# Stores in four transfers, and earlier loads of network vectors and bias rows, in a two-layer generated-weight convolution

## The chip, the cores and the metric

The kernel runs on one core of one Trainium2 chip. The metric is the device time of one execution in microseconds (us). "us" without more is a time of the profiled execution, counted from the start of its span.

## The reference, cut to what matters

Two layers of the same form follow each other. Each normalizes its input, makes a convolution kernel for every position from a small network, applies it, and adds the result and a bias to its input. Sizes: S = 32 samples, B = 32 chunks, C = 64 channels, L = 256 positions, A = 16, H = 128, all float32.

```python
x = x + conv(_gn(x), layer 0);  x = x + conv(_gn(x), layer 1)

def _gn(v, G=32, eps=1e-5):            # groups of 8 positions, over B and C too
    m, s = mean, var of v over (chunk, channel, 8 positions)
    return (v - m) / sqrt(s + eps)

def conv(x, z, W1, b1, g1, be1, W2, b2, Wb1, bb1, gb1, beb1, Wb2, bb2):
    h = relu(_ln(z @ W1 + b1, g1, be1))
    w = (h @ W2 + b2).reshape(B, L, CI, CO, K)       # K = 3 taps
    hb = relu(_ln(z @ Wb1 + bb1, gb1, beb1))
    bias = (hb @ Wb2 + bb2).transpose(0, 2, 1)
    x_uf = x padded by 1, three shifts stacked
    return einsum('sbilk,bliok->sbol', x_uf, w) + bias[None]
```

## The kernel before

**First stage** (`first_stats`, lines 223 to 290). The input goes through on-chip memory once, in 16 transfers of 4 MB, for the statistics of layer 0 (VectorE). Beside it 32 slots run the two small networks of both layers, two chunks per slot: class `Hidden` loads z (`zt`, line 163), projects (line 168), squares, sums and takes the root (ScalarE, GpSimd), transposes (line 195) and writes the hidden vectors to `hd` (line 201) and the bias rows to `bd` (line 216), both in device memory. All these transfers are issued by SyncE's queue (SP).

**Main loop** (lines 499 to 516). 64 units u (32 chunks in each of two layers) are done in two halves of the output channels, so that v = 2u + h runs from 0 to 127. In a half, TensorE makes the convolution kernels from `hT` (the hidden vectors of the unit, line 112) and `w2` in 12 groups (`make`, lines 418 and 419), and VectorE adds `b2` and puts them into `wall` (`take`, line 431). `products(v)` (lines 448 and 457) multiplies them with the normalized input `xn` and adds the result to the residual `ys[v % 3]`, in which GpSimd has added the bias rows `bt` to the input (`add_bias`, line 388). In layer 0 VectorE also takes the statistics of the result (line 460). After the first group of half v + 1 follow `products(v)` and then `after(v)`, in this order:

- `store(v)`: the finished half (1 MB, runs of 256 bytes) from `ys[v % 3]` to `x1` or `out`, issued by ScalarE's queue (line 397), in transfers of 8 partitions where u is even and of 4 where u is odd: 16 or 32 for a half.
- `normalize` (line 408): GpSimd subtracts `gmean` from `xt` into `xn`, and multiplies by `rstd` there.
- `load_pairs` (lines 122 and 123): the next input into `xt`, 2 MB in two transfers, SP. They wait for the subtraction, which reads `xt`.
- `load_residual(v + 3)` (line 131): 1 MB in four transfers, SP. Each waits for the stores that read the same part of the ring of three.
- `add_bias(v + 3)`: four transfers of `bt` (line 384, 1 MB written), SP, then the addition on GpSimd.

`load_hidden(u + 1)` (line 114, SP) stands at the start of the second half of unit u, behind all of this for the half before it. `hT` has two buffers, `bt` one.

What sets the order: instructions run in the order written on each engine, and a queue's issues wait in line. Besides the waits for data, each transfer is given one of eight semaphores (DMAHW0 to DMAHW7) in turn, over both queues together, and waits until the transfer that had the same semaphore before, eight transfers earlier, has landed.

Of the kernel before, what the change touches and what calls it, by code (L numbers as in the profile page):

```python
# [23 lines left out]
FP = mybir.dt.float32  # L24
# [17 lines left out]
def conv_layers(ctx: ExitStack, tc: tile.TileContext, x: bass.AP, layers: list, out: bass.AP):  # L42
# [18 lines left out]
    BLK = 2 * L  # L61
    NBLK = BLK // P
    RING = 3
    assert 2 * C == P and NT * S == P and M == P and BLK == 512 and EB == 2 * E
# [47 lines left out]
    def load_hidden(u):  # L112
        h = hp.tile([P, 2, M], FP, tag="hT", name="hT")
        nc.sync.dma_start(out=h, in_=hd[u // 2][u % 2].rearrange("p (a m) -> p a m", a=2))
        return h
# [41 lines left out]
    class Hidden:  # L157


        def __init__(self, stage, zts, small, i):  # L160
            n, j = divmod(i, B // 2)
            self.stage, self.i, self.t, self.zt = stage, i, small[n], zts[i % len(zts)]
            nc.sync.dma_start(out=self.zt[0:A], in_=layers[n]["z"][:, j * BLK : (j + 1) * BLK])

# [18 lines left out]
        def scale(self):  # L183
# [13 lines left out]
            for net, (g, be) in enumerate((("g1", "be1"), ("gb1", "beb1"))):  # L197
                nc.scalar.activation(  # L198
                    self.ht[:, net, :], p2[:, net, :], AF.Relu, bias=self.t[be], scale=self.t[g]
                )  # L200
            nc.sync.dma_start(
                out=hd[self.i].rearrange("b p f -> p b f"),
# [3 lines left out]
        def bias(self):  # L206
            p3 = ps_c.tile([C, BLK], FP, tag="pc", name="p3")
            nc.tensor.matmul(p3, self.t["Wb2"], self.ht[:, 1, :], start=True, stop=True)  # L208
            bs = self.stage.tile([C, 2, M, 2], FP, tag="bs", name="bs", bufs=2)
            nc.scalar.activation(  # L210
                bs.rearrange("o b m a -> o b a m"),
                p3.rearrange("o (b a m) -> o b a m", b=2, a=2),
                AF.Identity,
                bias=self.t["bb2"],
            )
            nc.sync.dma_start(
                out=bd[self.i].rearrange("b t o l -> o (b t) l"),
                in_=bs.rearrange("o b (t m) a -> o (b t) (m a)", t=NT),
            )
# [3 lines left out]
    def first_stats():  # L223
# [3 lines left out]
        with tc.tile_pool(name="stage", bufs=1) as stage:  # L227
# [14 lines left out]
            for j in range(2):  # L242
                zts.append(stage.tile([A + 1, BLK], FP, name=f"zt_{j}"))
                nc.vector.memset(zts[j], 1.0)
# [118 lines left out]
    with tc.manual_schedule():  # L363
# [13 lines left out]

        def add_bias(v):
            u, h = divmod(v, NH)
            y = residual(v)  # L380
            bt = bp.tile([P, CH, LT], FP, tag="bt", name="bt")
            for t in range(NT):
                src = bd[u // 2][u % 2, t, h * CH : (h + 1) * CH, :]
                nc.sync.dma_start(
                    out=bt[t * S : (t + 1) * S],
                    in_=bass.AP(src.tensor, src.offset, [[0, S]] + list(src.ap)),
                )
            nc.gpsimd.tensor_tensor(y, y, bt, ALU.add)  # L388

        def store(v):  # L390
            u, h = divmod(v, NH)
            to = x1[u] if u < B else out[:, u - B]

            n = 8 >> (u % 2)
            for t in range(NT):
                for s in range(0, S, n):
                    nc.scalar.dma_start(  # L397
                        out=to[s : s + n, h * CH : (h + 1) * CH, t * LT : (t + 1) * LT],
                        in_=residual(v)[t * S + s : t * S + s + n],
                    )  # L400

# [61 lines left out]

        hs[0] = load_hidden(0)
        normalize(0, 0)
        load_pairs(0, 1)
        normalize(0, 1)
        load_pairs(1, 0)
        add_bias(0)
        normalize(1, 0)  # L470
        load_pairs(1, 1)
        for v in range(1, RING):
            add_bias(v)

        def after(v):
# [16 lines left out]
            if v + RING < NH * U:  # L492
                load_residual(v + RING)
                add_bias(v + RING)

        before = None
        starts = range(0, CH, OG)
        order = [(2, o) for o in starts] + [(kind, o) for o in starts for kind in range(2)]
        for v in range(NH * U):
            u, h = divmod(v, NH)  # L500
            n = u // B
            if h == 1 and u + 1 < U:
                hs[u + 1] = load_hidden(u + 1)
# [52 lines left out]
```

## Time and profile before

| what | value |
|---|---|
| time, median of 3 runs | 6633.02 us (6631.62 to 6640.4) |
| time of the profiled execution | 6633.55 us, span 6631.8 us |
| granted TensorE clock, mean | 0.825 |
| TensorE matmuls busy | 4240.1 us (64%) |
| VectorE busy | 3272.9 us (49%) |
| GpSimd busy | 2051.9 us (31%) |
| ScalarE busy (without issues) | 117.9 us (2%) |
| mean busy share of the 16 DMA engines | 47.0% for SP's queue, 11.7% for ScalarE's |
| bytes moved | 785.21 MB, mean 118 GB/s |

The profile is of one execution. Issues of transfers are not counted as busy; they are rows of SPq and ACTq. No engine is busy for most of the span, and the 16 DMA engines are not either, so what to read is which waits stand one behind the other.

### The profile page before, as it was taken

To read this page: it belongs to the slowest core of one execution; us is meant where nothing else is said; L and a number is where in the kernel's file an instruction comes from. 1 tells how busy PE (TensorE), PEld (TensorE's weight loads), DVE (VectorE), ACT (ScalarE), POOL (GpSimd) and SP (SyncE) were. 2 spreads that over 40 slices of the span, in tenths; PEclk is the share of its full clock that TensorE was granted. 3 is DMA by queue.
4 is the path that set the end of the run, shared out by engine and by line. 5 is a ranking of instruction groups with operands and counts; after the bars stand their busy time and mean duration, and the time that the engine had idled before them with its cause. 6 is when DMAs were issued, how large, how long until landed. Compare 5 with 4: busy or idle time off the path is not lost.

```text
span 6631.8 us, 194874 instructions
## 1 busy us (share of the span) xinstructions
PE 4240.1 (64%) x90760; PEld 3965.6 (60%) x90760; DVE 3272.9 (49%) x3768; ACT 117.9 (2%) x181; POOL 2051.9 (31%) x618
## 2 busy tenths in 40 slices
PE   4657656765656765665674866666766666667765
PEld 2336656755655665565674766556766666666765
DVE  4545445644544654544563554445544454445544
ACT  2220000000000000000000000000000000000000
POOL 2224332323323323233231423333323333333322
PEclk7558888988888888888887888888988888888887
DMA  5556555565655656555556665656666665656664
GB/s 203 210 147 121 104 108 109 114 112 109 113 107 107 112 114 113 108 107 110 110 111 140 121 119 110 119 110 117 117 117 118 114 117 113 116 113 116 116 119 75
DMA packets 1407283, 785.21 MB, mean 118 GB/s; under 512 B 1107396, under 2 KB 1385992, under 8 KB 1387528
## 3 DMA queue, kind: packets, MB, share of 16 engines
q1 hardware_dynamic: 865800, 638.46, 47.0%
q10 hardware_dynamic: 540672, 134.28, 11.7%
q8 instruction: 711, 11.65, 0.8%
q14 instruction: 100, 0.82, 0.0%
HBM read 625.78 MB, written 146.80 MB: 116 GB/s over the span
## 4 chain that ended last, share of the span: by engine, by line
DMA 52%; POOL 17%; ACTq 14%; PE 8%; SPq 3%; issue 2%; DVE 2%; ACT 1%; POOLq 0%; DVEq 0%
DMA room<-in_x_dram 15%; ACTq L397 14%; DMA room<-x 13%; DMA bt<-bd 8%; POOL xn L408 8%; POOL room L388 7%; DMA x<-room 6%; DMA out_dram<-room 5%; PE pc L448 3%; DMA hT<-hd 2%; PE pg L418 2%; PE p L168 2%; DVE wall L431 2%; DMA zt<-in_L_conv_z_dram 2%; POOL sq L180 1%
## 5 line engine op out<-in xcount | busy, mean ns | idle before, releaser
L418 PE MATMUL pg<-hT,w2t 128*64 128x128 f32 x24576 | 2958.8, 282 | 1858.7 <-DMA hT<-hd 1639.4
L418 PEld LDWEIGHTS pg<-hT,w2t 128*64 128x64 f32 x24576 | 2815.9, 142 | 1970.1 <-issue 1766.8
L419 PE MATMUL pg<-hT,w2t 128*64 128x128 f32 x24576 | 2967.0, 283 | 102.2 <-issue 101.9
L419 PEld LDWEIGHTS pg<-hT,w2t 128*64 128x64 f32 x24576 | 2815.9, 143 | 102.3 <-issue 102.0
L431 DVE TENSOR_TENSOR wall<-pg,b 64x1024 f32<-64x1024 f32 (+1 forms) x2048 | 2486.3, 1221 | 513.7 <-PE pg L419 487.1
L388 POOL TENSOR_TENSOR room<-room,bt 128x2048 f32<-128x2048 f32 x128 | 579.9, 4531 | 4052.8 <-DMA out_dram<-room 1458.2
L457 DVE TENSOR_TENSOR room<-pc,room 128x512 f32<-128x512 f32 x512 | 353.9, 691 | 2527.1 <-PE pc L448 2352.2
L448 PE MATMUL pc<-wall,xn 128*32 128x128 f32 (+2 forms) x40960 | 1016.4, 259 | 115.6 <-issue 92.1
L448 PEld LDWEIGHTS pc<-wall,xn 128*32 128x32 f32 x40960 | 971.2, 114 | 175.6 <-issue 148.7
L408 POOL TENSOR_TENSOR xn<-xn,rstd 128x2048 f32<-128x2048 f32 x128 | 758.2, 5923 | 10.0
L408 POOL TENSOR_TENSOR xn<-room,gmean 128x2048 f32<-128x2048 f32 x128 | 601.3, 4698 | 53.5 <-ACT gmean L361 29.4
L168 PE MATMUL p<-wc,zt 17*128 17x256 f32 x256 | 120.2, 647 | 208.7 <-DMA zt<-in_L_conv_z_dram 208.7
L168 PEld LDWEIGHTS p<-wc,zt 17*128 17x128 f32 x256 | 79.7, 326 | 236.5 <-DMA zt<-in_L_conv_z_dram 158.0
L180 POOL TENSOR_TENSOR sq<-sq 128x512 f32<-128x512 f32 (+2 forms) x192 | 103.6, 539 | 363.1 <-ACT sq L172 350.6
L460 DVE BATCH_NORM_STATS2 between<-room 128x6 f32<-128x256 f32 x512 | 192.8, 418 | 8.7
L195 PEld LDWEIGHTS p<-ident,hs 128*128 128x128 f32 x256 | 49.6, 221 | 55.3 <-issue 41.4
L184 DVE RECIPROCAL var<-var 128x8 f32<-128x8 f32 x32 | 6.3, 196 | 133.7 <-ACT var L181 133.4
L195 PE MATMUL p<-ident,hs 128*128 128x128 f32 x256 | 61.2, 419 | 4.6 <-DVE hs L186 4.6
L208 PE MATMUL p<-ht,Wb 128*64 128x512 f32 x64 | 63.0, 1088 | 1.6 <-ACT ht L198 1.6
L271 DVE BATCH_NORM_STATS2 parts<-xn 128x6 f32<-128x256 f32 x192 | 64.0, 408 | 0.0
L346 ACT ACTIVATE nv<-nv,eps 128x8 f32<-128x8 f32 x1 | 0.3, 300 | 3161.4 <-DMA x<-room 3161.4
L271 DVE BATCH_NORM_STATS2 parts<-room 128x6 f32<-128x256 f32 x160 | 53.4, 409 | 0.0
(61 smaller groups left out, 319.0 us busy)
## 6 DMA issues: line engine op xcount, KB each, us to landing
bt<-bd SPq DMA_DIRECT2D x512, 256.0 KB
room<-in_x_dram SPq DMA_DIRECT2D x64, 1024.0 KB
room<-in_x_dram SPq DMA_DIRECT2D x256, 256.0 KB
room<-x SPq DMA_DIRECT2D x64, 1024.0 KB
room<-x SPq DMA_DIRECT2D x256, 256.0 KB
room<-in_x_dram SPq DMA_DIRECT2D x64, 1020.0 KB
room<-x SPq DMA_DIRECT2D x64, 1020.0 KB
x<-room ACTq DMA_DIRECT2D x512, 64.0 KB
```

Source lines behind the costliest of these rows:

```text
L168: nc.tensor.matmul(self.p1[:, k], self.zt[:, k * P : (k + 1) * P], self.t["wc"], start=True, stop=True)
L180: nc.gpsimd.tensor_tensor(to, self.sq[:, :, 0:w], self.sq[:, :, w : 2 * w], ALU.add)
L271: return lambda: nc.vector.bn_stats(parts[:, q % NJ, g, :], xs[q % NX][:, :, g * E : (g + 1) * E])
L388: nc.gpsimd.tensor_tensor(y, y, bt, ALU.add)
L397: nc.scalar.dma_start(out=to[s : s + n, h * CH : (h + 1) * CH, t * LT : (t + 1) * LT], in_=residual(v)[t * S + s : t * S + s + n],)
L408: nc.gpsimd.tensor_tensor(o, i, b, op)
L418: nc.tensor.matmul(pg[0:C, k, :], w[:, k0 * C : (k0 + 1) * C], h0, start=True, stop=True)
L419: nc.tensor.matmul(pg[C:P, k, :], w[:, k1 * C : (k1 + 1) * C], h1, start=True, stop=True)
L431: nc.vector.tensor_tensor(at(wall[rows, 0, a : a + 1], [[WT, NT], [F, MT], [1, OG]]), pg[rows].rearrange("p o (t m) -> p t m o", t=NT), b2 ...
L448: nc.tensor.matmul(pc[t * S : (t + 1) * S, n0 - q * EB : n1 - q * EB, :], xn[:, u % 2, t * MT + p + 1, :], wall[:, t, a : a + (n1 - n0) * CH],
L457: nc.vector.tensor_tensor(part, pc.rearrange("p n o -> p o n"), part, ALU.add)
L460: nc.vector.bn_stats(between[:, 2 * q + g, u, h, :], part[:, :, g * E : (g + 1) * E])
```

## The change

Four things are changed.

- `store(v)` issues four transfers of 32 partitions for each half, for all u, still from ScalarE's queue.
- `load_hidden(u + 1)` is issued by ScalarE's queue, and at the start of the first half of unit u, one half earlier.
- `add_bias` is split: `load_bias(v)` issues the four transfers of `bt` (SP), and now stands behind `add_bias(v - 1)`, whose reading of the one `bt` buffer it waits for. So the bias rows of a half are loaded ahead of its pairs and residual.
- In the first stage z is loaded for two slots at once (64 KB) and one such block ahead, and z, `hd` and `bd` are issued by ScalarE's queue.

```diff
     def load_hidden(u):
-        nc.sync.dma_start(out=h, in_=hd[u // 2][u % 2]...)
+        nc.scalar.dma_start(out=h, in_=hd[u // 2][u % 2]...)
...
-            n, j = divmod(i, B // 2)
-            self.stage, self.i, self.t, self.zt = stage, i, small[n], zts[i % len(zts)]
-            nc.sync.dma_start(out=self.zt[0:A], in_=layers[n]["z"][:, j * BLK : (j + 1) * BLK])
+            self.stage, self.i, self.t = stage, i, small[i // (B // 2)]
+            zt = zts[i // ZB % len(zts)]
+            for b in [0, 1] if i == 0 else [i // ZB + 1] if i % ZB == 0 else []:
+                if b * ZB < U // 2:
+                    n, j = divmod(b * ZB, B // 2)
+                    nc.scalar.dma_start(
+                        out=zts[b % len(zts)][0:A], in_=layers[n]["z"][:, j * BLK : (j + ZB) * BLK]
+                    )
+            self.zt = zt[:, i % ZB * BLK : (i % ZB + 1) * BLK]
...
-            nc.sync.dma_start(
+            nc.scalar.dma_start(
                 out=hd[self.i].rearrange("b p f -> p b f"),
...
-            nc.sync.dma_start(
+            nc.scalar.dma_start(
                 out=bd[self.i].rearrange("b t o l -> o (b t) l"),
...
-        def add_bias(v):
+        bts = {}
+
+        def load_bias(v):
             u, h = divmod(v, NH)
-            y = residual(v)
-            bt = bp.tile([P, CH, LT], FP, tag="bt", name="bt")
+            bts[v] = bp.tile([P, CH, LT], FP, tag="bt", name="bt")
             for t in range(NT):
                 src = bd[u // 2][u % 2, t, h * CH : (h + 1) * CH, :]
                 nc.sync.dma_start(
-                    out=bt[t * S : (t + 1) * S],
+                    out=bts[v][t * S : (t + 1) * S],
...
-            nc.gpsimd.tensor_tensor(y, y, bt, ALU.add)
+
+        def add_bias(v):
+            y = residual(v)
+            nc.gpsimd.tensor_tensor(y, y, bts.pop(v), ALU.add)
...
-            n = 8 >> (u % 2)
             for t in range(NT):
-                for s in range(0, S, n):
-                    nc.scalar.dma_start(
-                        out=to[s : s + n, h * CH : (h + 1) * CH, t * LT : (t + 1) * LT],
-                        in_=residual(v)[t * S + s : t * S + s + n],
-                    )
+                nc.scalar.dma_start(
+                    out=to[:, h * CH : (h + 1) * CH, t * LT : (t + 1) * LT],
+                    in_=residual(v)[t * S : (t + 1) * S],
+                )
...
             if v + RING < NH * U:
                 load_residual(v + RING)
                 add_bias(v + RING)
+            if v + RING + 1 < NH * U:
+                load_bias(v + RING + 1)
...
-            if h == 1 and u + 1 < U:
+            if h == 0 and u + 1 < U:
                 hs[u + 1] = load_hidden(u + 1)
```

How the rows move is shown at two places. ScalarE's queue, unit 1, second half, before: the first six of the 32 stores (`x_1_73` is `x1` of unit 1, `room` holds the ring; the words in brackets are what the row waits for).

```order
L397 DMA x_1_73<-room 4x32x64 [waits DMAHW4_49,DVE_49,Pool_49]
L397 DMA x_1_73<-room 4x32x64 [waits DMAHW6_49]
L397 DMA x_1_73<-room 4x32x64 [waits DMAHW1_49]
L397 DMA x_1_73<-room 4x32x64 [waits DMAHW4_49]
L397 DMA x_1_73<-room 4x32x64 [waits DMAHW5_49]
L397 DMA x_1_73<-room 4x32x64 [waits DMAHW7_49]
```

The same place now: `hT` of the next unit, then all four stores of the half, then the next unit.

```order
L115 DMA hT<-hd_105 128x256 [waits DMAHW2_49,PE_49]
L405 DMA x_1_73<-room 32x32x64 [waits DMAHW1_49,DMAHW5_49,DVE_49,Pool_49]
L405 DMA x_1_73<-room 32x32x64 [waits DMAHW3_49,DMAHW0_49]
L405 DMA x_1_73<-room 32x32x64 [waits DMAHW2_49]
L405 DMA x_1_73<-room 32x32x64 [waits DMAHW7_49,DMAHW4_49]
L405 DMA x_2_74<-room 32x32x64 [waits DMAHW3_49,DMAHW5_49,DVE_49,Pool_49]
```

Each store still waits for a semaphore of an earlier transfer, but there are four such waits for a half where there were 32, and `hT` has come in ahead of them.

SP's queue at the seam of two halves of early units, before: the last residual transfer, the four of `bt`, `hT`, and the next pair and residual loads.

```order
L131 DMA room<-in_x_dram 32x32x64 [waits DMAHW5_49,DMAHW4_49,DMAHW6_49,DMAHW3_49,DMAHW7_49,DMAHW2_49,DMAHW1_49]
L384 DMA bt<-bd_138 32x2048 x4
L114 DMA hT<-hd_106 128x256 [waits DMAHW1_49,PE_49]
L122 DMA room<-in_x_dram 64x16x256 [waits DMAHW3_49,Pool_49]
L123 DMA room<-in_x_dram 64x16x255 [waits DMAHW5_49]
L131 DMA room<-in_x_dram 32x32x64 [waits DMAHW2_49,DMAHW7_49,DMAHW0_49,DVE_49]
```

The same seam now.

```order
L132 DMA room<-in_x_dram 32x32x64 [waits DMAHW6_49]
L392 DMA bt<-bd_138 32x2048 [waits DMAHW3_49,DMAHW7_49,DMAHW1_49,Pool_49]
L392 DMA bt<-bd_138 32x2048 [waits DMAHW0_49]
L392 DMA bt<-bd_138 32x2048 [waits DMAHW1_49]
L392 DMA bt<-bd_138 32x2048 [waits DMAHW2_49]
L123 DMA room<-in_x_dram 64x16x256 [waits DMAHW3_49,Pool_49]
L124 DMA room<-in_x_dram 64x16x255 [waits DMAHW5_49]
L132 DMA room<-in_x_dram 32x32x64 [waits DMAHW7_49,DVE_49]
```

The rows of `bt` stand between the same loads as before, but belong to the half after the one whose residual stands above them, and the first of them now waits for GpSimd (Pool), that is for the addition that reads `bt`. `hT` is gone from this queue, and a residual transfer waits for one or two semaphores where it waited for up to seven.

## Rows read from the trace of the kernel before

**Rows 1.** The page: chain by line; products: busy us, mean ns, idle.

```profile
DMA room<-in_x_dram 15%; ACTq L397 14%; DMA room<-x 13%; DMA bt<-bd 8%; POOL xn L408 8%; POOL room L388 7%; DMA x<-room 6%; DMA out_dram<-room 5%; PE pc L448 3%; DMA hT<-hd 2%; PE pg L418 2%; PE p L168 2%; DVE wall L431 2%; DMA zt<-in_L_conv_z_dram 2%; POOL sq L180 1%
...
L448 PE MATMUL pc<-wall,xn 128*32 128x128 f32 (+2 forms) x40960 | 1016.4, 259 | 115.6 <-issue 92.1
```

**Rows 2.** Waits of the span: total us, times, longest us.

```profile
PE pg L418 <- DMA hT<-hd: 1639.4, 63, 43.6
PE p L168 <- DMA zt<-in_L_conv_z_dram: 208.7, 31, 46.9
```

**Rows 3.** Chain from 3079 to 3180: start us, duration us, what.

```profile
3079.73 4.65 POOL xn L408
...
3085.04 13.04 DMA room<-in_x_dram
...
3098.10 0.25 ACTq L397
...
3114.34 3.39 DMA x<-room
...
3119.25 7.71 DMA bt<-bd
...
3129.89 4.51 POOL room L388
3134.40 4.69 POOL xn L408
...
3139.76 13.03 DMA room<-in_x_dram
...
3162.79 9.81 DMA bt<-bd
...
3177.29 4.65 POOL xn L408
```

**Rows 4.** Windows: stretch, engines busy, then clock, DMA share, GB/s.

```profile
3100.00:3106.00 6.00, 0.00 (x0) 0.00 (x0) 0.00 (x0) 0.00 (x0) 0.00 (x0) 0.50 0.25 46
3152.50:3155.50 3.00, 3.00 (x60) 3.00 (x58) 2.97 (x3) 0.00 (x0) 0.00 (x0) 1.00 1.21 153
3123.00:3127.00 4.00, 0.00 (x0) 0.00 (x0) 0.00 (x0) 0.00 (x0) 0.00 (x0) 0.50 1.06 246
0.00:490.00 490.00, 253.82 (x640) 152.28 (x640) 240.24 (x685) 115.60 (x178) 110.69 (x230) 0.62 0.56 189
```

**Rows 5.** Timeline of SP's queue: start, duration, what was issued.

```profile
3014.87 0.34 SPq L114 DMA_DIRECT2D hT<-hd  x1
...
3085.94 32.24 SPq L131 DMA_DIRECT2D room<-in_x_dram  x4
```

**Rows 6.** Timeline of VectorE: first addition of products in four halves.

```profile
3564.42 0.69 DVE L457 TENSOR_TENSOR room<-pc,room 128x512 f32<-128x512 f32 x1 [2.52 <-DMA x<-room]
...
3597.40 0.69 DVE L457 TENSOR_TENSOR room<-pc,room 128x512 f32<-128x512 f32 x1 [2.52 <-DMA x<-room]
...
6531.68 0.69 DVE L457 TENSOR_TENSOR room<-pc,room 128x512 f32<-128x512 f32 x1 [42.12 <-DMA out_dram<-room]
...
6562.62 0.69 DVE L457 TENSOR_TENSOR room<-pc,room 128x512 f32<-128x512 f32 x1 [2.52 <-PE pc L448]
```

**Rows 7.** Timeline of GpSimd: start of the loop, and some bias additions.

```profile
491.88 3.51 POOL L373 MEMSET wall<- 64x4096 f32 x1 [14.93 <-DMA hT<-hd]
...
624.70 4.55 POOL L388 TENSOR_TENSOR room<-room,bt 128x2048 f32<-128x2048 f32 x1 [28.15 <-DMA x<-room]
...
3623.01 4.49 POOL L388 TENSOR_TENSOR room<-room,bt 128x2048 f32<-128x2048 f32 x1 [34.49 <-DMA bt<-bd]
...
3725.57 4.52 POOL L388 TENSOR_TENSOR room<-room,bt 128x2048 f32<-128x2048 f32 x1 [20.39 <-DMA hT<-hd]
...
6544.99 4.54 POOL L388 TENSOR_TENSOR room<-room,bt 128x2048 f32<-128x2048 f32 x1 [5.14 <-DMA bt<-bd]
```

**Rows 8.** Chain of the first stage: first load of x.

```profile
5.17 12.94 DMA xn<-in_x_dram
```

More of the change, by code (lines that the diff above doesn't have):

```diff
@@ L62, in conv_layers @@
     NBLK = BLK // P
+    ZB = 2
     RING = 3
@@ L113, in load_hidden @@
         h = hp.tile([P, 2, M], FP, tag="hT", name="hT")
-        nc.sync.dma_start(out=h, in_=hd[u // 2][u % 2].rearrange("p (a m) -> p a m", a=2))
+        nc.scalar.dma_start(out=h, in_=hd[u // 2][u % 2].rearrange("p (a m) -> p a m", a=2))
         return h
@@ L242, in first_stats @@
             for j in range(2):
-                zts.append(stage.tile([A + 1, BLK], FP, name=f"zt_{j}"))
+                zts.append(stage.tile([A + 1, ZB * BLK], FP, name=f"zt_{j}"))
                 nc.vector.memset(zts[j], 1.0)
@@ L464, in conv_layers @@
         hs[0] = load_hidden(0)
+        load_bias(0)
         normalize(0, 0)
@@ L469, in conv_layers @@
         add_bias(0)
+        load_bias(1)
         normalize(1, 0)
@@ L473, in conv_layers @@
             add_bias(v)
+            load_bias(v + 1)
         def after(v):
```

## The prediction

> **What bounds the kernel now.** I read the chain of work that ended last first. Transfers lead it: pair and residual loads (room), 15% and 13%, the issues of the stores on ScalarE's queue, 14%, bias rows 8%, stores 6% and 5%, and GpSimd's two lines, 8% and 7%, while TensorE's lines have some 7% [rows 1]. The list of waits seems to say something else: TensorE waited 1639.4 us in 63 waits for hT, 26 us for each unit [rows 2]. SP's queue shows why: the issue of hT takes 0.34 us and stands behind everything else that SP has to issue for the half before [rows 5]. So hT is late because SP's line is late. TensorE runs into that line; it does not draw it, and 1639 us is not what the change can give.
>
> The line itself is a loop that closes once for each half. GpSimd subtracts the mean (4.65), which frees xt; the pair loads go and land (13.04 from the issue of the second one); stores follow until 3117.7, because the four residual issues wait for the stores piece by piece (SP's four took 32.24 us, [rows 5]); then the bias rows (from 3119.25), then the addition on GpSimd (4.51), and the next subtraction begins at 3134.40. That loop took 54.7 us in a half with 32 stores (3079.73 to 3134.40) and 42.9 in one with 16 (3134.40 to 3177.29) [rows 3]. From the addition at 624.70 to that at 6544.99 there are 124 loops; one, at the change of layer, takes 102.6 (3623.01 to 3725.57) [rows 7], so the other 123 have a mean of (5920.3 - 102.6) / 123 = 47.3 us.
>
> What would TensorE and VectorE need if nothing held them? Two undisturbed halves tell: 33.0 us from one first addition to the next in layer 0, 30.9 in layer 1 [rows 6]. A mean of 31.9 is the floor of a half.
>
> **The stores.** Transfers of four partitions move 46 GB/s when alone and keep 0.25 of the DMA engines busy [rows 4]; on all engines that would be 184 GB/s. So 1.05 MB takes 5.7 us of all engines where it took 23. The 32 or 16 issues, each waiting for its semaphore's turn, become four. The stretch from the landed pair loads to the last bias issue, 3098.1 to 3119.2, 21 us [rows 3], was theirs; what remains of it is the residual transfer. That has no row of its own in the loop, since it was spread over the waits for stores; a window in which little else moves has 153 GB/s [rows 4], so 1.05 MB takes 6.9 us. The waits by turns don't vanish: with 14 or 15 transfers for each half, the one eight earlier is, for a store, mostly a residual or bias transfer of the half before. A store can therefore go when those land, which is when GpSimd starts to add and the engines would rest.
>
> By that, one store in four runs in this rest and three beside loads: 3/4 of 5.7, 4.2 us, with bounds 0 (all in the rest) and 5.7 (none). [...]
>
> **The bias rows.** Their stretch of 7.7 us at the end of the loop (9.8 in the other half [rows 3]) goes: the rows for a half are asked for when the addition before has ended, and move at 246 GB/s [rows 4], 4.3 us, while GpSimd subtracts. Added is a wait of SP for the addition. Behind it stand the pair loads, which wait for the subtraction that follows the same addition anyway, so the wait itself costs nothing. The bytes do cost: 7.7 us from issue to landing against 4.69 of subtraction and 0.67 until the second pair issue leaves 2.35 at most, 0 at least. I take 1.5, as most of the four have moved before the last is issued.
>
> **hT.** It leaves SP's line and TensorE gets it a half earlier. It now waits on ScalarE's queue for the matmuls that read the older buffer, and the stores of the half before stand behind it; those need products that TensorE makes later still, so nobody waits longer. Its gain is inside the loop's gain: without it the loop's stores would start late for half of the halves. 0 beyond that.
>
> **The loop's sum.** Subtraction 4.69, issue 0.67, pair loads 13.03, residual 6.9, addition 4.51: 29.8. Bias 1.5, stores 4.2: 35.5 us. That is above the floor of 31.9, so the loop still bounds, and 123 x (47.3 - 35.5) = 1451 us go. The half of 33.0 in layer 0 comes near, and TensorE's wait should be small there.
>
> **The first stage** ended at 491.88 [rows 7]. TensorE waited 208.7 us in it for z [rows 2]. One block ahead, these waits go; not all becomes time. The stage moves 189 GB/s x 490 us = 92.6 MB [rows 4]; at the rate of the first load of x, 4.19 MB in 12.94 us [rows 8], 324 GB/s, it can't end before 286 us. VectorE is busy for 240 us of it [rows 4] and stops at each merging of statistics. ScalarE now issues hd and bd between its activations, and where these wait for a semaphore of a 4 MB load or, at the end, of the residual loads, its arithmetic waits too. Between 60 and 200 us go; I take 130.
>
> **The rest.** Start of the loop, change of layer and end have the same serial parts with fewer stores: the last store alone, 32 transfers of 1 us, shrinks by some 15. I take 50 for all three, between 0 and 80.
>
> **Rivals.** (1) *TensorE becomes the bound.* If the stores fit into the rest, a loop needs 29.8 to 31.3 and the floor of 31.9 holds: 123 x 15.4 = 1894, and 6633.6 - 1894 - 180 = 4560 us. For it: the stores need only cost under 2.1 us of the loop. Against: only a store whose turn comes with the last residual piece meets idle engines, and that is one of four. (2) *Stores come beside the loads and are waited for.* The stores are 256-byte runs like the residual; if they take turns with it, packet by packet, all of 5.7 lies on the path, and a residual piece that waits for its store to land comes later by the rest of a landing (3.4, as the last store in [rows 3]), with bias at its 2.35: 29.8 + 5.7 + 3.4 + 2.35 = 41.3, 738 us go, 6633.6 - 738 - 180 = 5716. It would be so if TensorE were late with products, which the 31.9 against 35.5 speaks against. (3) *Slower than before.* The place is the chain of turns: a store waits for the residual of the half before, a residual for its store, the bias for the addition, and the pair loads and the next store for these. If nothing of it overlaps and TensorE, left with no lead, makes the products in between (1016.4 us of matmuls for 128 halves, 7.9 each [rows 1]), a loop takes 29.8 + 7.7 + 5.7 + 3.4 + 7.9 = 54.5 and the time is 6633.6 + 123 x 7.2 - 180 = 7339. It decides from a loop of 47.3 + 180 / 123 = 48.8 on. Against: TensorE has half a loop of lead even now, when it waits. (4) *Only hT and the first stage change*, the stores being held by their turns as before: the stretch from landed pair loads to the last bias issue stays, 21.1 us and 10.0 us in turn (3098.1 to 3119.2, 3152.8 to 3162.8), the bias goes, and the landing of 3.4 and the 1.5 come in its place: 4.69 + 0.67 + 13.03 + 15.6 + 3.4 + 1.5 + 4.51 = 43.4, 480 us go, 6633.6 - 480 - 180 = 5974.
>
> **How the numbers follow.** Against the profiled execution, 6633.55 (its span and 1.75 us around it; 0.5 above the median): 6633.6 - 1451 - 130 - 50 = 5002, said as 5000. Chances: the forecast, loop 33.5 to 38.5, 0.53; rival 1, 0.20; rival 2, 0.18; rival 3, 0.03; rival 4, 0.05; 0.01 for a cause that leaves no change. The range holds rival 1 at its time and part of what lies between the forecast and rival 2: from 4460 (loop 31.9, 200 from the first stage, 80 from the rest) to 5570, midway between the upper ends together (bias 2.35, stores 5.7, loop 37.9, 60 from the first stage, none from the rest: 5417) and rival 2. About 0.2% is what a measurement of this kernel can tell from no change. Faster by more: 0.96; within: 0.01; slower: 0.03.
>
> **What would show it.** The starts of the bias addition on GpSimd should be 33 to 38 us apart and no longer alternate between 43 and 55. TensorE's wait for hT should be gone; in its place products wait for residuals or xn, if I am right, or the additions wait for products, if rival 1 is. SP's four residual issues should take under 10 us; if they still take 20, stores bind. In the chain, bias rows and ACTq should be nearly gone and pair loads lead. The first stage should end near 360. I am wrong if loops stay above 40, above all with stores of four partitions' rate.

## The result, and the profile after

The changed kernel takes 5457.18 us (median of 4 runs, 5455.9 to 5476.56) where the kernel before takes 6632.32 in the same comparison: a ratio of 0.8237, 95% interval 0.8214 to 0.826. That is 1175 us less; the forecast was 1632 less, and the range held the time. The question is why the loop stopped short, and the experiments found more behind it than that.

The page of the changed kernel: engines' busy time, the queues, the chain by engine and by line, and the group of the products (its line, L448 in [rows 1], is L456 now).

```profile
PE 4322.6 (79%) x90760; PEld 4033.9 (74%) x90760; DVE 3269.2 (60%) x3768; ACT 118.1 (2%) x181; POOL 2034.0 (37%) x618
...
q1 hardware_dynamic: 829960, 616.43, 59.8%
...
q8 instruction: 711, 11.65, 1.0%
...
PE 41%; POOL 17%; DVE 16%; DMA 13%; issue 10%; SPq 2%; ACT 0%; POOLq 0%; ACTq 0%; DVEq 0%
PE pc L456 23%; DVE wall L439 13%; POOL xn L416 11%; PE pg L426 10%; PE pg L427 5%; POOL room L399 5%; DMA room<-x 5%; DMA room<-in_x_dram 4%; DMA out_dram<-room 2%; SPq L132 2%; DMA x<-room 2%; PE p L175 1%; DVE room L465 1%; DVE parts L278 1%; PE p L215 1%
...
L456 PE MATMUL pc<-wall,xn 128*32 128x128 f32 (+2 forms) x40960 | 1261.8, 289 | 761.6 <-issue 424.6
```

TensorE, not the transfers, now leads the chain, and GpSimd comes second. The products are busy longer than before (1261.8 us against 1016.4) with the same 40960 matmuls, and the idle time ahead of them has grown from 115.6 to 761.6. Both are losses that the sum did not hold. The list of waits (total us, times, longest) names two kinds:

```profile
PE pc L456 <- issue: 424.6, 204, 6.2
...
PE pc L456 <- POOL xn L416: 335.2, 62, 8.2
PE p L175 <- DMA zt<-in_L_conv_z_dram: 32.6, 1, 32.6
...
PE pg L426 <- DMA hT<-hd: 7.9, 1, 7.9
```

The wait for hT (1639.4 in [rows 2]) has gone to 7.9, that for z from 208.7 to 32.6. In their place TensorE waits in 62 of 64 units for xn, the normalized input, and 204 times for nothing that a semaphore shows ("issue"). GpSimd's timeline gives the parts of the gain: the first clearing of wall, the fourth addition, those at the change of layer, and the last.

```profile
312.97 3.51 POOL L380 MEMSET wall<- 64x4096 f32 x1 [18.16 <-DMA room<-in_x_dram]
...
422.35 4.59 POOL L399 TENSOR_TENSOR room<-room,bt 128x2048 f32<-128x2048 f32 x1 [19.98 <-DMA room<-in_x_dram]
...
2866.85 4.52 POOL L399 TENSOR_TENSOR room<-room,bt 128x2048 f32<-128x2048 f32 x1 [21.91 <-DMA room<-x]
...
2946.53 4.55 POOL L399 TENSOR_TENSOR room<-room,bt 128x2048 f32<-128x2048 f32 x1 [14.96 <-DMA room<-x]
...
5407.56 4.59 POOL L399 TENSOR_TENSOR room<-room,bt 128x2048 f32<-128x2048 f32 x1 [3.42 <-DMA room<-x]
```

Set against [rows 7]: the first stage ends 178.9 us earlier (491.88 to 312.97). The 123 loops go from 47.3 to (5407.56 - 422.35 - 79.68) / 123 = 39.9 us, 912 us in all. The loop at the change of layer shrinks from 102.6 to 79.7, the start of the loop by 23.4 (132.8 to 109.4), the end by 39.6 (86.8 to 47.2, from the last addition to the end of the span): 86 for these three. The sum is 1177, the difference of the two spans.

Where the 39.9 come from is seen in one unit, halves 53 and 54. The chain of work in order of time (start, duration, what):

```profile
2449.66 0.70 DVE room L465
2450.42 3.08 DMA x<-room
2453.52 0.33 SPq L132
2453.89 1.91 SPq L132
2455.85 7.54 DMA room<-in_x_dram
...
2463.64 4.55 POOL room L399
2468.18 4.65 POOL xn L416
2472.90 5.70 POOL xn L416
2478.64 6.29 PE pc L456 x182
2484.93 4.85 issue
2489.78 4.52 PE pc L456 x105
2494.32 0.70 DVE room L465
```

Products of half 53 end, the half is stored, a residual is loaded, GpSimd adds the bias rows to it, normalizes, and only then do the products of half 54 begin: 29.0 us in a row (2449.66 to 2478.64). The residual here is that of half 54. Its place in the ring was emptied by the store of half 51, two halves before that of half 53, so by its data it could have gone long before. SP's queue shows that its first piece did:

```profile
2425.36 0.67 SPq L124 DMA_DIRECT2D room<-in_x_dram  x1
2426.71 31.14 SPq L132 DMA_DIRECT2D room<-in_x_dram  x4
...
2474.28 14.78 SPq L132 DMA_DIRECT2D room<-in_x_dram  x4
```

The first piece was issued at 2426.71; the four took 31.14 us. In the order in which the program gives out the eight semaphores, the second piece of residual 54 comes eight places behind the first piece of store 53. The program gives that piece no other wait, so it is held by a store that TensorE had not yet made possible. In the trace both carry the same one of the eight (number 103 there), and the piece left at 2453.52, when that store, issued at 2450.42, had landed. Of the 1992 transfers in the trace, 1240 can be set against the landing of the one before on their semaphore; not one of their issues ended ahead of it. SP's own list of waits has one such wait in each unit, in every second half:

```profile
SPq L132 <- DMA x<-room: 751.0, 32, 26.6
SPq L132 <- DMA out_dram<-room: 714.5, 32, 26.9
```

In the half between, where the four issues took 14.78 us, no store stands one turn ahead of the residual. And GpSimd works in written order (the addition at 2463.64 above, the normalization from 2468.18), so the normalization stands behind the addition that waits for this residual: the pair loads that it needs were issued at 2424.71 and 2425.36, and GpSimd then stood idle for 34.07 us, up to the addition at 2463.64.

The second loss is in the products that follow this wait. Windows of TensorE: quiet products (half 53), the wait ahead of half 54, its products (columns as in [rows 4]):

```profile
2439.00:2450.00 11.00, 8.65 (x331) 7.93 (x331) 4.68 (x10) 0.00 (x0) 0.00 (x0) 1.00 0.21 32
2474.00:2478.50 4.50, 0.00 (x0) 0.00 (x0) 0.00 (x0) 0.00 (x0) 4.50 (x1) 0.69 0.92 188
2478.50:2494.50 16.00, 11.01 (x319) 10.66 (x320) 4.51 (x10) 0.00 (x0) 0.37 (x2) 0.77 0.96 147
```

The same 320 matmuls take 11 us in one half and 16 in the next. In the second, TensorE had stood still for 4.9 us, the granted clock had fallen (0.50 from 2476 to 2482), the DMA engines were full (0.96 against 0.21), and in the middle stands a pause of 4.85 us. Of the 5 us more, 2.5 are pauses (4.85 against 2.36 in three) and the rest is slower matmuls.

### The profile page after: what moved, and what is told of

Same layout as the page of the kernel before. It is cut to its first block, busy times and chain, and to the rows that moved or that the text cites. A ratio compares the mean times of both kernels' runs of the same rounds, so it can differ in the third digit from the quotient of the medians.

```text
span 5454.8 us, 191315 instructions
## 1 busy us (share of the span) xinstructions
PE 4322.6 (79%) x90760; PEld 4033.9 (74%) x90760; DVE 3269.2 (60%) x3768; ACT 118.1 (2%) x181; POOL 2034.0 (37%) x618
## 2 busy tenths in 40 slices
DMA packets 1398552, 784.94 MB, mean 144 GB/s; under 512 B 1098949, under 2 KB 1377545, under 8 KB 1378825
## 3 DMA queue, kind: packets, MB, share of 16 engines
q1 hardware_dynamic: 829960, 616.43, 59.8%
q8 instruction: 711, 11.65, 1.0%
## 4 chain that ended last, share of the span: by engine, by line
PE 41%; POOL 17%; DVE 16%; DMA 13%; issue 10%; SPq 2%; ACT 0%; POOLq 0%; ACTq 0%; DVEq 0%
PE pc L456 23%; DVE wall L439 13%; POOL xn L416 11%; PE pg L426 10%; PE pg L427 5%; POOL room L399 5%; DMA room<-x 5%; DMA room<-in_x_dram 4%; DMA out_dram<-room 2%; SPq L132 2%; DMA x<-room 2%; PE p L175 1%; DVE room L465 1%; DVE parts L278 1%; PE p L215 1%
## 5 line engine op out<-in xcount | busy, mean ns | idle before, releaser
L426 PE MATMUL pg<-hT,w2t 128*64 128x128 f32 x24576 | 2814.8, 274 | 249.6 <-DVE wall L439 200.3
L426 PEld LDWEIGHTS pg<-hT,w2t 128*64 128x64 f32 x24576 | 2682.6, 137 | 355.3 <-PE pg L427 263.8
L427 PE MATMUL pg<-hT,w2t 128*64 128x128 f32 x24576 | 2825.5, 275 | 29.7 <-issue 29.6
L427 PEld LDWEIGHTS pg<-hT,w2t 128*64 128x64 f32 x24576 | 2682.5, 137 | 32.3 <-issue 32.1
L456 PE MATMUL pc<-wall,xn 128*32 128x128 f32 (+2 forms) x40960 | 1261.8, 289 | 761.6 <-issue 424.6
L456 PEld LDWEIGHTS pc<-wall,xn 128*32 128x32 f32 x40960 | 1188.3, 129 | 843.5 <-issue 494.4
L416 POOL TENSOR_TENSOR xn<-xn,rstd 128x2048 f32<-128x2048 f32 x128 | 741.0, 5789 | 10.0
L175 PE MATMUL p<-wc,zt 17*128 17x256 f32 x256 | 108.3, 593 | 33.4 <-DMA zt<-in_L_conv_z_dram 32.6
L215 PE MATMUL p<-ht,Wb 128*64 128x512 f32 x64 | 61.6, 1065 | 10.6 <-ACT ht L205 10.6
L278 DVE BATCH_NORM_STATS2 parts<-spare 128x6 f32<-128x256 f32 x160 | 53.4, 408 | 0.0
```

What stands on the lines that cost most here:

```text
L175: nc.tensor.matmul(self.p1[:, k], self.zt[:, k * P : (k + 1) * P], self.t["wc"], start=True, stop=True)
L278: return lambda: nc.vector.bn_stats(parts[:, q % NJ, g, :], xs[q % NX][:, :, g * E : (g + 1) * E])
L416: nc.gpsimd.tensor_tensor(o, i, b, op)
L426: nc.tensor.matmul(pg[0:C, k, :], w[:, k0 * C : (k0 + 1) * C], h0, start=True, stop=True)
L427: nc.tensor.matmul(pg[C:P, k, :], w[:, k1 * C : (k1 + 1) * C], h1, start=True, stop=True)
L456: nc.tensor.matmul(pc[t * S : (t + 1) * S, n0 - q * EB : n1 - q * EB, :], xn[:, u % 2, t * MT + p + 1, :], wall[:, t, a : a + (n1 - n0) * CH],
```

## The experiments

Each run stands beside a run of the kernel before on the same chip; ratios compare across runs. Apart from the rows of the kernel before, the changed one and the residual on ScalarE's queue, each is a single execution. That last kernel gave 0.7087 on one chip and 0.7035 on another, so a difference of some 0.005 says nothing. Waits are TensorE's, in us: for xn, for hT, and within the products for no semaphore ("pauses").

| kernel | time, us | ratio | xn | hT | pauses |
|---|---|---|---|---|---|
| before | 6632.3 | 1 | 8.7 | 1639.4 | 92.1 |
| changed | 5457.2 | 0.8237 | 335.2 | 7.9 | 424.6 |
| stores undone | 5870.6 | 0.8888 | 664.5 | 7.7 | 461.7 |
| bias rows undone | 5856.8 | 0.8840 | 421.6 | 7.9 | 693.9 |
| first stage undone | 5634.0 | 0.8504 | 329.5 | 2.3 | 425.4 |
| hT undone | 5390.6 | 0.8162 | 4.6 | 322.0 | 428.5 |
| stores alone | 5300.7 | 0.8000 | 8.5 | 424.1 | 54.3 |
| addition one half later | 5007.1 | 0.7581 | 10.0 | 7.2 | 361.4 |
| the same, residual in long runs | 4970.9 | 0.7503 | 9.1 | 4.6 | 349.5 |
| residual on ScalarE's queue | 4658.1 | 0.7035 | 11.5 | 8.3 | 103.6 |
| the same, 0.98 MB more per unit | 4720.9 | 0.7125 | 19.8 | 4.5 | 167.7 |
| the same, 2 KB more per unit | 4653.2 | 0.7023 | 17.5 | 4.5 | 112.8 |
| the same, stores undone | 6124.7 | 0.9243 | 896.4 | 81.9 | 394.3 |

### The wait by turns

**Residual loads on ScalarE's queue**, behind the stores of the same part of the ring.

```diff
-    def load_residual(v):
+    def load_residual(v, queue=nc.sync):
...
-            nc.sync.dma_start(
+            queue.dma_start(
                 out=residual(v)[t * S : (t + 1) * S],
...
-                load_residual(v + RING)
+                load_residual(v + RING, nc.scalar)
```

> One edit to the changed kernel: the loop's residual loads are issued by ScalarE's queue, right behind the stores of the same part of the ring, instead of by SP's. Theory A (turns): in every second half the residual of a later half waits, through the turn of the eight semaphores, for a store that was made only just now, GpSimd's addition waits for it, the normalization stands behind that addition, and the products behind that; on ScalarE's queue the residual waits for its own store, two halves older, and the chain opens. Then TensorE's wait for xn (335 us in 62) goes below 50 us, the products of 16 us become 9 to 10, a half takes 33.5 to 35.5 and the time is 4750 to 4950 us. Theory B (TensorE's own pauses between products, with DMA engines busy beside them, are what holds): the wait for xn goes but the pauses of 4 to 6 us stay, 37 us for a half, 5050 to 5200 us. Theory C (the ring of three is too short, the residual waits for its own store): nothing changes, 5400 to 5500 us.

A single execution took 4681.1 us. For more of them was expected:

> The same edit as in the first run with residual loads from ScalarE's queue (4681 us), timed in three rounds: 4670 to 4700 us, 0.705 to 0.712 of the time of the kernel before.

4658.09 us (4 runs, 4649.43 to 4668.61), ratio 0.7035, interval 0.7021 to 0.705, faster than both ranges expected. Theory A holds in its mechanism: the wait for xn is 11.5 us in all. The page's chain by engine, and its group of the products:

```profile
PE 61%; DVE 27%; issue 7%; DMA 2%; POOL 2%; ACT 1%; SPq 0%; ACTq 0%; DVEq 0%; POOLq 0%
...
L456 PE MATMUL pc<-wall,xn 128*32 128x128 f32 (+2 forms) x40960 | 1000.8, 255 | 117.9 <-issue 103.6
```

The timeline of ScalarE's queue, two halves:

```profile
1604.44 4.62 ACTq L405 DMA_DIRECT2D x<-room  x4
1609.15 14.86 ACTq L132 DMA_DIRECT2D room<-in_x_dram  x4
1636.99 6.50 ACTq L405 DMA_DIRECT2D x<-room  x4
1650.14 5.74 ACTq L132 DMA_DIRECT2D room<-in_x_dram  x4
```

The timeline of VectorE, the first addition of products in three halves:

```profile
1596.88 0.69 DVE L465 TENSOR_TENSOR room<-pc,room 128x512 f32<-128x512 f32 x1 [2.52 <-PE pc L456]
...
1630.49 0.69 DVE L465 TENSOR_TENSOR room<-pc,room 128x512 f32<-128x512 f32 x1 [2.52 <-PE pc L456]
...
1662.73 0.69 DVE L465 TENSOR_TENSOR room<-pc,room 128x512 f32<-128x512 f32 x1 [2.52 <-PE pc L456]
```

A residual now follows its own store, nearly three halves ahead of its use. That its place behind the pair loads on SP's queue had not been what held it is seen above: its first piece left 1.35 us after the second pair issue. Nor did the residual's 31.14 us on that queue hold the loads behind it: GpSimd did, since the bias rows left at 2468.21 and the next pair load at 2472.85, as its addition and its subtraction ended. First additions of products are 33.6 and 32.2 us apart, and the mean loop by GpSimd's additions is 33.2: about the floor of [rows 6], with the clock at 0.965. No byte more or less was moved (784.94 MB in both); what the edit changed is which transfer waits for which, and that was worth 799 us. The pauses fell with the wait for xn: beside the products the DMA engines are now busy to 0.27 and 0.26 in the mean of the two kinds of halves, where the changed kernel had 0.94 and 0.28.

**The addition one half later.** GpSimd adds for v + 2 instead of v + 3 behind half v.

```diff
-            add_bias(v)
-            load_bias(v + 1)
+            if v + 1 < RING:
+                add_bias(v)
+                load_bias(v + 1)
...
             if v + RING < NH * U:
                 load_residual(v + RING)
-                add_bias(v + RING)
-            if v + RING + 1 < NH * U:
-                load_bias(v + RING + 1)
+            if v + RING - 1 < NH * U:
+                add_bias(v + RING - 1)
+            if v + RING < NH * U:
+                load_bias(v + RING)
```

> One edit to the changed kernel: GpSimd adds the bias rows of half v + 2, not of v + 3, after half v (the residual is still loaded for v + 3, the bias rows one half later with the addition), so that the next normalization no longer stands behind an addition whose residual is still on its way. Theory A (GpSimd's written order puts the normalization behind the residual): the wait for xn goes below 50 us although the residual loads wait as long as before; 4750 to 4950 us. Theory B (pauses of TensorE): 5050 to 5200 us. A third way: the pair loads now wait by turns for the last stores, and take the place of the addition: 5300 to 5600 us.

5007.07 us, between the ranges of A and B. The wait for xn is gone (10.0), as A says, but A's condition, residual loads that wait as long as before, did not hold. SP's own list of waits:

```profile
SPq L132 <- DMA hT<-hd: 903.3, 59, 19.0
...
SPq L132 <- DMA x<-room: 44.9, 5, 24.3
```

With the bias rows loaded one half later the turns have moved as well: the residual now waits for hT, and hardly for stores (44.9 us here and 2.4 for those to `out`, where the changed kernel had 1465.5). So this run does not show by itself that GpSimd's order is part of the chain; the 34.07 us of GpSimd in the changed kernel above do. The pauses stay at 361.4, and the loop is 36.4.

### The parts undone, one at a time

**Stores** again in transfers of 8 and 4 partitions:

```diff
+            n = 8 >> (u % 2)
             for t in range(NT):
-                nc.scalar.dma_start(
-                    out=to[:, h * CH : (h + 1) * CH, t * LT : (t + 1) * LT],
-                    in_=residual(v)[t * S : (t + 1) * S],
-                )
+                for s in range(0, S, n):
+                    nc.scalar.dma_start(
+                        out=to[s : s + n, h * CH : (h + 1) * CH, t * LT : (t + 1) * LT],
+                        in_=residual(v)[t * S + s : t * S + s + n],
+                    )
```

> The changed kernel with the stores alone undone (transfers of 8 or 4 partitions again, 16 or 32 for a half). If the four-transfer stores carry most of the gain: 6000 to 6400 us, additions alternating between some 40 and 55 us, and SP's residual issues over 25 us. If hT and the early bias rows carry it: 5500 to 5700 us.

5870.55 us, between the two expectations: 0.065 of the time of before, 432 us, hang on the stores when the rest is changed.

**hT** from SP again, at the start of the second half:

```diff
-        nc.scalar.dma_start(out=h, in_=hd[u // 2][u % 2]...)
+        nc.sync.dma_start(out=h, in_=hd[u // 2][u % 2]...)
...
-            if h == 0 and u + 1 < U:
+            if h == 1 and u + 1 < U:
```

> The changed kernel with hT alone undone (issued by SP at the start of the second half of a unit, behind that half's residual and bias rows). The prediction gave hT nothing beyond the loop's own gain: 5440 to 5500 us. The rival: SP's residual issues still wait some 27 us for stores just made, hT stands behind them and TensorE waits 10 to 20 us for it in each unit: 6000 to 6700 us, with a wait for hT of 600 to 1200 us in the list.

5390.56 us, below what either expected, by 0.0075 of the time of before or some 50 us: hardly more than the 0.005 between two chips, so a gain is not shown. What is clear are the waits. TensorE waits 322.0 us for hT, as the rival said in kind, but the wait for xn is gone. The turns tell why: with hT back in SP's line each transfer is given another semaphore, and the second piece of residual 54 then stands one turn behind store 52, not 53. SP still waits for stores as long as before (747.5 us in 32 waits and 716.1 in 31), but for one a half earlier, and no longer in TensorE's way. The early hT took one wait from TensorE and, by shifting the turns, gave it another.

**Bias rows** again behind the residual of their own half (`load_bias` called inside `add_bias`, the other calls dropped):

> The changed kernel with the early bias rows alone undone (loaded behind the residual of their own half, as before). If their 7.7 to 9.8 us come back in each loop less the 1.5 that they cost now: 123 times 6 to 8 us, 6150 to 6450 us. If they stand in line only in every second half, where the addition holds the normalization: 62 times 8 us, 5900 to 6000 us. If something else hides them: below 5550 us.

5856.76 us, just below the second expectation, but its reason, a place in line in every second half, is little of it. The residual still waits for the store just made (its last piece now), and the wait for xn, again 62 times, grew by 86 us (421.6). The pauses grew by 269 (693.9). In the changed kernel the products of the halves that do not wait for xn ran beside quiet DMA engines and took 10.6 us in the mean; here the engines are full beside the products of both kinds (mean share 1.00 and 1.06), and both take some 16.

**First stage** again with z for one slot at a time, and z, `hd` and `bd` from SP:

> The changed kernel with the first stage alone undone (z for one slot at a time, not ahead, z, hidden vectors and bias rows issued by SP). The first stage ended 179 us earlier with the change (312.97 against 491.88), so 5600 to 5660 us if that is this part of the change alone, with GpSimd's first clearing of wall back near 490 us; under 5550 us if part of the 179 us came from elsewhere.

5633.95 us, as expected, with GpSimd's first clearing of wall at

```profile
491.34 3.51 POOL L374 MEMSET wall<- 64x4096 f32 x1 [14.72 <-DMA bd<-bs]
```

So the 179 us of the first stage are this part of the change, and beside the other three they simply add.

**The stores alone**, the kernel before with nothing else changed:

> The kernel before with the stores in four transfers as its only change. With the other three changes made, undoing the stores cost some 430 us. If the parts add: 6150 to 6250 us. If the stores by themselves open the line and the others only follow: 5800 to 6000 us. If hT and the bias rows, still behind the residual on SP's queue, take the gain back: 6400 to 6600 us.

5300.66 us, better than any of the three: 0.2000 of the time goes by this one part, 1326 us, where all four together bring 1175 and the first stage's 177 are among these. If the first stage adds here too, hT early and bias rows early cost some 330 us together where the stores go in four. In this kernel the residual of half 54 stands one turn behind store 52, as with hT undone, TensorE does wait for hT, and its products fall into a quiet time (the DMA engines beside them busy to 0.13 and 0.05 in the mean):

```profile
L446 PE MATMUL pc<-wall,xn 128*32 128x128 f32 (+2 forms) x40960 | 1009.2, 258 | 80.4 <-issue 54.3
...
PE pg L416 <- DMA hT<-hd: 424.1, 63, 10.9
```

**Fine stores with the residual on ScalarE's queue:**

> The kernel with residual loads on ScalarE's queue (4658 us), its stores in 16 and 32 transfers again. Theory A (what the stores cost was the chain from a store through the residual, the addition and the normalization to the next products, and with the residual two halves ahead that chain is open): most of the price of small stores is hidden now, 4700 to 5000 us, products waiting less than 100 us for xn. If the stores' own rate (46 GB/s when alone) binds ScalarE's queue whatever stands behind: 5400 us and more.

6124.65 us. Theory A falls at this place: I had thought that with the residual two halves ahead nothing would be left of the stores' price. The second expectation's time holds. On this queue the issues themselves are the line, 46.42 us for 32 stores (an estimate from the 46 GB/s of [rows 4] gives 23 us for them), with the residual and hT behind them:

```profile
1568.18 33.45 ACTq L407 DMA_DIRECT2D x<-room  x27
1601.72 6.01 ACTq L132 DMA_DIRECT2D room<-in_x_dram  x4
1607.77 1.43 ACTq L115 DMA_DIRECT2D hT<-hd  x1
1609.30 46.42 ACTq L407 DMA_DIRECT2D x<-room  x32
1655.81 4.83 ACTq L132 DMA_DIRECT2D room<-in_x_dram  x4
```

So the residual's place on ScalarE's queue is worth something with four stores; with 16 and 32 it costs 0.0355 of the time of before (0.9243 against 0.8888).

### The pauses between products

**Long runs.** The kernel with the late addition, its residual read in other places of the same array, in runs of 8 KB:

```diff
-                in_=source(u)[:, h * CH : (h + 1) * CH, t * LT : (t + 1) * LT],
+                in_=source(u)[:, h * CH + t * CH // NT : h * CH + (t + 1) * CH // NT, :],
```

> The kernel with the late addition (5007 us; its products pause 2 to 3 us at a place about every 128 multiplications), with the loop's residual loads reading the same megabyte in runs of 8 KB or more instead of 256 bytes. The numbers then stand at wrong places of the residual, nothing else changes. Theory P (the pauses are fetches of TensorE's instructions that stand behind the many small packets of the residual on the DMA engines): the pauses fall below 1 us, the products take 8 to 9 us and the time is 4650 to 4850 us. Rival Q (the bytes count, not the packets) or R (pauses have nothing to do with the residual loads): products of 10 to 12 us and pauses stay, 4950 to 5030 us.

4970.9 us, with pauses of 349.5 against 361.4. The packets of SP's queue fell from 829960 to 322056 and the pauses hardly moved. Theory P, small packets, falls; between Q and R the run does not decide.

**More traffic.** The kernel with the residual on ScalarE's queue, and one store behind each hT, of 0.98 MB or of 2 KB:

```diff
+    side = dram.tile([P, 10 * K * C], FP, name="side")
+    def side_store():
+        nc.scalar.dma_start(out=side, in_=w2[:, 0:10, :].rearrange("p i o -> p (i o)"))
...
                 hs[u + 1] = load_hidden(u + 1)
+                side_store()
```

> The kernel with residual loads on ScalarE's queue (4658 us) and one transfer added for each unit, which nobody waits for: 0.98 MB of w2, unchanged, stored to a spare place in device memory, issued by ScalarE's queue right behind hT, that is, as the products of a unit's second half begin. The products of the first halves see nothing of it. Theory T (a pause between two products is a wait for TensorE's next block of instructions, which comes through the same DMA engines and is late when these are full): the products of the second halves take 10.5 to 13 us instead of 8 and hold a pause of 2 to 5 us, those of the first halves stay at 7.3 to 8.5; the time is 4770 to 4950 us. Theory N (pauses have nothing to do with traffic): both kinds stay, 4640 to 4720 us.

> The same as the run with the added store of 0.98 MB, but the added transfer has 2 KB: as many transfers and the same turns of the semaphores, no traffic. Under both theories 4640 to 4720 us and products as without it; anything longer is the price of the turn, not of the bytes.

4720.85 and 4653.24 us. The 2 KB cost nothing, the megabyte 68 us. The place is as theory T says, the size is not: the time lies between the ranges of N and T. Over the whole run the products beside the added megabyte took 9.6 us in the median against 8.4 with 2 KB, those of the other halves 8.3 in both. In ten units from 1500 us on, products beside the added megabyte took 10.1 us in the median (7.6 to 12.9) where with 2 KB they took 8.2 to 9.4 and once 12.3 in six units, and those of the other halves stayed at 7.3 to 8.6; expected were 10.5 to 13. One unit shows how. The timeline of TensorE, the products beside an added store that was issued at 1883.32:

```profile
1884.51 3.58 PE L461 MATMUL pc<-wall,xn 128*32 128x32 f32 x145
...
1889.63 2.88 PE L461 MATMUL pc<-wall,xn 128*32 128x96 f32 x128 [1.54 <-issue]
...
1895.02 2.36 PE L461 MATMUL pc<-wall,xn 128*32 128x128 f32 x47 [2.51 <-issue]
```

The DMA queues there, first from 1884 to 1887, then from 1887 to 1888 (packets, MB, share of 16 engines):

```profile
q10 hardware_dynamic: 261, 1.09, 90.5%
...
q8 instruction: 1, 0.02, 5.8%
q10 hardware_dynamic: 1, 0.00, 0.1%
```

While the store ran (90.5% of all engines), no block of the instruction queue came; one came in the microsecond after it. The second pause, 2.51 us, is not the store's: the bias rows on SP's queue then filled the engines (102.5% from 1890 to 1892), and the next block came from 1892 to 1893. Pauses are 128 matmuls apart. The page counts 711 such blocks, 11.65 MB in all, for 90760 matmuls and as many weight loads. My estimate from these counts, if all the blocks are TensorE's, is 255 instructions a block, so that 128 matmuls with their loads would be one block. In the changed kernel the quiet products of half 53 had three blocks in 8 us; in the 8 us from 2478 the SP queue held 117.6% of the engines and there was none, and one came at 2486 to 2489, in the pause of 4.85 us. The whole trace says the same: in the changed kernel TensorE went on after each of the 204 pauses of more than 0.2 us in its products 1.2 to 1.8 us after such a block had landed, and so it did after each of the 128 with the residual on ScalarE's queue. So I read a pause as a wait for a block; no semaphore shows it. That the block comes late where the engines are full is what the added megabyte shows, with products of 9.6 us against 8.4. It is not all of it: with the residual in long runs the engines beside the products were busy to 0.27 and 0.35 only, and the products still took 11.0 and 11.6 us; why, stays open.

## Why the prediction was right, and where it was not

**What bounds, before.** That transfers and not TensorE drew the line was right, and that the 1639 us for hT were not the gain. The loop fell short by 123 x (39.9 - 35.5) = 541 us, of which the first stage and the rest gave back 85. The range held the time by its stretch towards rival 2: the sum's own upper ends gave 5417, and 5457 lies beyond them.

**Stores.** GpSimd's pieces of the line came as summed (addition 4.55, subtraction 4.65). The transfers did not: the first of four stores landed 3.08 us after its issue, but their megabyte ran on beside the residual up to 2460, some 9 us where the sum had 4.2, and the residual's last three pieces took 9.9 (2453.52 to 2463.39) where all four had 6.9. The failed step is the sentence on the turns: I asked what a *store* waits for, a residual or bias transfer of the half before, and never what a *residual* waits for. In every second half it is the store just made. So the loop is not the 35.5 of the sum, which pair loads lead; it closes over two halves and holds TensorE's work and, between the products of its two halves, the 29.0 us of store, residual, addition and normalization, of which TensorE's making of the next kernels covers all but some 5.

**The rivals.** The measured 39.9 lies beyond the forecast's 33.5 to 38.5 and short of rival 2's 41.3. Rival 2's mechanism is what came, stores waited for with their landing in the line, in one half of two; rival 3's point, TensorE left without lead, came in the same half. I spoke against it with the half loop of lead that TensorE had before; the turns took that lead away. Beside the kernel with the residual on ScalarE's queue, whose loop takes 33.2, the changed one loses 6.7 us a half. By the lists that is (335.2 - 11.5) / 128 = 2.5 of wait for xn, (424.6 - 103.6) / 128 = 2.5 of pauses and (1261.8 - 1000.8) / 128 = 2.0 of slower matmuls, some 7 together. For the last two the sum had no term: its floor of 31.9 comes from two undisturbed halves.

**hT.** "0 beyond that" holds for the time, as far as one run tells (some 50 us the other way), but as the sum of two effects: a wait for hT of 314 us less and one for xn of 331 more. I had followed its wait, its data and its queue, not the turns of the others, which it moves.

**Bias rows.** Undone, they cost 400 us, but only where hT has moved too. With neither moved, the stores alone less the first stage's 177 would take 5124 (an estimate that adds two runs), and with the bias rows early and hT not, it is 5391: there they cost some 270.

**First stage.** 130 forecast, 60 to 200 as range, 178.9 measured: mis-sized, with the mechanism right (the wait for z went from 208.7 to 32.6). **The rest** measured 86 where I took 50, up to 80.

**What would show it.** The additions still alternate, 30 and 50 us apart; the four residual issues took 31.14 and 14.78, and "if they still take 20, stores bind" named the fault. The mean loop of 39.9 stays a hair below the 40 that was to show me wrong; every second loop is above it. The chain has lost its bias rows and ACTq, as said, but pair loads do not lead it.

## What to carry to other kernels

Where transfers take semaphores in turn, as here, a load can be held by a transfer that has nothing to do with its data (SP's residual issues waited 1465.5 us for stores), and moving any one transfer shifts the turns of all the others (with hT back on SP's queue the wait for xn went from 335.2 to 4.6 us): for each load that an engine will need, look up which transfer stands one full turn ahead of it, and whether that one depends on work not yet done. A load that refills a buffer can stand on the queue of the store that empties it, directly behind it; here that one line took the kernel from 5457 to 4658 us, but with 16 and 32 stores a half, which fill that queue, it lost (5871 to 6125). And changes to several waits at once should be run apart: one of the four here was worth more alone than all four together.

## What the runs showed of the hardware

The page of the changed kernel counts a queue of 711 instruction blocks on the same 16 DMA engines as the data (11.65 MB, 16384 bytes each in the trace, 1.0% of the engines' span). If they are TensorE's, as the estimate of 255 matmuls and weight loads to a block and the pauses at every 128 matmuls suggest, the products, 320 matmuls with their weight loads, use 2.5 of them in 8 us. The products paused 0.5 to 1.1 us three times in the quiet half 53 and 4.85 us in half 54 with the engines full. Each pause over 0.2 us of the changed kernel ended 1.2 to 1.8 us after a block had landed. The kernel before paused for 92.1 us in all, the changed one for 424.6, the one with stores alone for 54.3.

In half 54 the loss came twice: the granted clock was at 0.50 when its products began, 4.9 us after TensorE had stopped, at 0.50 again from 2490 to 2492, behind the pause of 4.85 us, and at 1.00 in the quiet half.
